# A mixture-of-experts combination and a state-space preparation inside an attention loop: each of their operations is tied to an attention unit, and their tiles move from PSUM banks to SBUF

## The chip, the cores and the metric

The kernel runs on one core of a Trainium2 chip. A core has five engines, each with its own in-order queue: PE (TensorE, matmuls), DVE (VectorE), ACT (ScalarE), POOL (GpSimd) and SP (SyncE, which here only issues DMAs). They meet at semaphores. SBUF is the working memory, PSUM holds eight banks of 128 x 512 float32 that PE writes and ACT and DVE read. The metric is the device time of one execution in microseconds, as the median of several runs.

## The reference, cut to what matters

A tensor `x` of 4 elements (the batch) by 1024 tokens by 128 features goes through four layers. Each layer is an attention-like block and a feed-forward block, each with a residual and a layer norm behind it. The change lies in the third layer and at the start of the fourth:

```
# third layer: attention (16 heads of 64), causal, relu features times cos and sin
x = layernorm(x + cosformer(x))
# third layer: mixture of experts, top 2 of 8
probs = softmax(x @ router.T); weights, indices = top_k(probs, 2)
weights = weights / (weights.sum() + 1e-6)
y = sum over the 2 chosen of weights * (silu(x @ gate_e) * (x @ up_e)) @ w2_e
x = layernorm(x + y)
# fourth layer: a selective state-space block
xn = x * rsqrt(mean(x*x) + 1e-5) * norm_w
xs = silu(conv4(xn @ in_w.T) + conv_b)           # 256 channels, 4 taps along time
delta = softplus(xs @ wd1.T @ wd2.T + wd2_b)
h[t] = exp(delta[t] * A) * h[t-1] + delta[t] * xs[t] * Bm[t]   # 16 states per channel
y[t] = sum over states of h[t] * Cm[t]
```

## The kernel before

Everything is float32. The four elements live in SBUF as `xN[b]` (tokens on partitions, 8 chunks of 128 tokens) and `xT[b]` (features on partitions). The program is written as Python generators that are advanced in turn; a scheduler with a timeline model then fixes the order of each engine's queue, moving an operation ahead of others on its engine where it holds it to be ready. Inside the attention loop PE's order alone is kept as written (`manual_schedule`).

**The attention loop** (`l2_attn`, L947) runs over 128 units: 4 elements x 4 quarters of 256 tokens x 8 pairs of heads. A unit's steps are spread over neighbouring turns `t`: `l2_project` (L1070) makes queries and keys with two PE matmuls into a bank `pqk` and two ACT activations `r_q`, `r_k` (L1078), and POOL turns the queries (`qt`, L1086); `l2_keys` transposes the keys (`kN`, L1101); `l2_scores` multiplies keys by queries into `pa_m` and DVE masks them (`a`, L1144); `l2_sums` updates the running state (matmuls into `kp_mo`, DVE `st`, L1125 and L1128); `l2_before` and `l2_within` accumulate `po` (L1153); `l2_out` divides on DVE (`dn`, `co`, L1196 to L1198). Every fourth unit `l2_project_out` transposes `co` into a bank `pt`, copies it with ACT (`coT`, L1220) and multiplies it by the output weights (`pr`, L1223). At the end of an element there is a layer norm (`norm_parts`, L162, whose Sqrt on ACT, L177, needs a table load, L177, and another, L1517, for the Tanh after it), a router and the expert dispatch.

PSUM in the loop: two rotating banks with the tag `pj` serve `pqk`, the values `pv`, the transposes `pt`, the router and everything of the early preparation below; `po` has two banks' width, `pr` one, and three shared banks hold scores, states and the experts' `ph` and `py`. PE waits for a `pj` bank until its last reader is done.

**The experts** (`l2_ffn`, L1429, the generator `moe`) start inside the attention loop as soon as an element's rows are dispatched: one expert tile of 128 rows per turn (`sg`, `mh` on DVE and ACT, L1517 to L1521, `ys`, L1537). When an element's 23 tiles are done, its **combination** `l2_combine` (L1546) follows: two halves of 4 chunks. For each half POOL issues 8 indirect DMAs that gather the two expert rows of each token (`yg`, L1556), ACT scales each of the 8 tiles of 128 x 128 by its weight (L1573, L1580), DVE adds them and the residual (L1583, L1585), and `norm_parts` makes the layer norm.

**The early preparation** (`l3_early`, L1721, and `l3_prepare`, L1745) makes the first half (512 tokens of element 0) of the fourth layer ready while the attention of element 3 still runs. It starts when element 0's combination is done, and advances by one step per unit (L1014 to L1018). Steps: squares, Sqrt and scaling (L1754 to L1761); a transpose and `xnT`; for each of two channel groups a matmul `pxe`, a four-tap convolution on DVE that reads the bank four times (L1786, L1792), three small operations for the next half's edge (`tail`), Tanh back into the bank (L1806), and `xs` (L1807); a matmul `pdb` and the store of 32 rows to DRAM; then, for each group, softplus: a matmul `pd`, Abs and a maximum, Exp, plus one, minus one back into the bank, Ln, three additions in the bank and a product on DVE (L1837 to L1840), and a copy out of the bank (L1841).

**The fourth layer** (`l3`, L1622) scans 8 halves of 512 tokens; for each of 16 states POOL multiplies (`db`, L1876), ACT takes the exponential (`da`, L1880), DVE scans (L1881), POOL multiplies again (`hc`, L1892) and PE sums in `pys`. The remaining expert tiles, the combinations of elements 1 to 3 and the last feed-forward block (`ph`, `hh`, `py`) run beside it.

The attribute `self.beat` is set in `l2_project` to the ACT instruction that makes the newest `r_k`. Before the change only the dispatch's scatters use it: they get a dependency on the beat, so that they can't be scheduled ahead of the unit at which they are written.

Of the kernel before, what the change touches and what calls it, by code (L numbers as in the profile page):

```python
# [42 lines left out]
E3, NST, DDELTA, KCONV = 256, 16, 64, 4  # L43
# [28 lines left out]
class Net:  # L72
# [874 lines left out]
    def l2_attn(self, load, dispatch, moe, first):  # L947
# [5 lines left out]
        nc, tc = self.nc, self.tc  # L953
        NQ = 2
        with ExitStack() as ctx:
# [35 lines left out]
            for t in range(-2, n + 4):  # L991
                if t == 0:
                    load()
                if 0 <= t + 1 < n:
                    u = units[t + 1]
                    if u["hp"] == 0:
                        i = (t + 1) // NP2
                        if i + 1 < len(quarters):
                            nxt = quarters[i + 1]
                            self.l2_tiles(nxt, quarters[i])  # L1000
                            side.append(self.l2_values(nxt))
                    self.l2_keys(u)
# [522 lines left out]
    def l2_expert_out(self, u, units, i, wp):  # L1525
# [12 lines left out]
        if j % 4 == n - 1:  # L1538
# [4 lines left out]
                in_=ys[:, 0:n, :],  # L1543
            )

    def l2_combine(self, st, wp):  # L1546

        nc, b = self.nc, st["b"]
        yg = {}

        def gather(h, c):
# [169 lines left out]
    def l3_early(self, pool):  # L1721


        half = lambda b, i: self.xT[b][:, i * 512 : (i + 1) * 512]
        k = [0]

        def at(name, shape):
            if name in ("xnT", "tail", "xs3"):
                return pool.tile(shape, F32, name=name)
            if name in ("dl", "ud"):  # L1730
# [8 lines left out]
            return half(0, name == "sp_w")[:, None, :]  # L1739

        u = dict(b=0, h=0, at=at, ff=self.bank("pj"))
        self.c3["first"] = u
        return u

    def l3_prepare(self, u):  # L1745
# [2 lines left out]
        at, ff, dp = u.get("at", self.l3_at), u.get("ff", self.bank("ff")), c3["dp"]  # L1748
        wdb = c3["we"][:, :, 0:ND]

        sq = at("sq3", [P, 4, D])
        ms = self.sm.tile([P, 4], F32, name="ms3")
        for k in range(4):
            nc.scalar.activation(  # L1754
                sq[:, k, :], self.xN[b][:, 4 * h + k, :], AF.Square, accum_out=ms[:, k : k + 1]
            )
        yield
        nc.scalar.activation(ms, ms, AF.Sqrt, bias=self.epsc, scale=1.0 / D)
        nc.vector.reciprocal(ms, ms)
        for k in range(4):  # L1760
            nc.scalar.activation(  # L1761
                sq[:, k, :], self.xN[b][:, 4 * h + k, :], AF.Copy, scale=ms[:, k : k + 1]
            )
        yield
        pt = ff([P, 4, P], "pt")
        for k in range(4):
            self.tr(pt[:, k, :], sq[:, k, :])
# [2 lines left out]
            xnT, pt.rearrange("p a b -> p (a b)"), AF.Copy, scale=self.col("norm_w")  # L1770
        )
        yield

        K1 = KCONV - 1
        tail = at("tail", [P, 2, K1]) if h == 0 else u["prev"]["tail"]
# [2 lines left out]
        for ec in range(2):  # L1778
            p = ff([P, 512], "pxe")
            self.mm(p, c3["wskip"][:, 1, ec * P : (ec + 1) * P], xnT)  # L1780
            xc = at("xc", [P, 512])
# [4 lines left out]
            nc.vector.tensor_scalar(xc[:, o:], p[:, o:], w[K1], bias, ALU.mult, ALU.add)  # L1786
            if h:
                nc.vector.scalar_tensor_tensor(
                    xc[:, 0:K1], p[:, 0:K1], w[K1], tail[:, ec, :], ALU.mult, ALU.add
                )  # L1790
            for d in range(1, KCONV):
                nc.vector.scalar_tensor_tensor(  # L1792
                    xc[:, d:], p[:, 0 : 512 - d], w[K1 - d], xc[:, d:], ALU.mult, ALU.add
                )
# [11 lines left out]
            nc.scalar.activation(p, xc, AF.Tanh)  # L1806
            nc.vector.scalar_tensor_tensor(xs[:, ec, :], p, 1.0, xc, ALU.add, ALU.mult)  # L1807
# [9 lines left out]
        yield  # L1817

        dl, ud = at("dl", [P, 2, 512]), at("ud", [P, 2, 512])
        for g in ((0,), (1,)) if "at" in u else ((0, 1),):  # L1820
            us, v = at("sp_u", [P, len(g), 512]), at("sp_w", [P, len(g), 512])
            p2 = []
            for k, ec in enumerate(g):
# [11 lines left out]
            for k, ec in enumerate(g):  # L1835
# [6 lines left out]
            if g[-1] == 0:  # L1842
                yield
        u.update(xnT=xnT, xs=xs, dl=dl, ud=ud, rows=rows)

    def l3_scan(self, u):
# [400 lines left out]
```

## Time and profile before

| | |
|---|---|
| median of 3 runs | 2261.67 us (2253.73 to 2262.74) |
| profiled execution | 2265.2 us; its span (first to last instruction) 2263.4 us |
| mean granted TensorE clock | 0.934 |
| PE, DVE, ACT, POOL busy | 1988.1, 1361.8, 1184.6, 1025.0 us |
| first two layers | 0 to 593 us: PE busy 505.95 us |
| attention loop of the third layer | 593 to 1303 us: PE busy 652.14 of 709.60 us |
| from there to the first `db` of the scan | 1303 to 1363.5 us: PE busy 35.82 of 60.50 us |
| scan stage | 1363.5 to 2130 us: PE 673.13, POOL 675.18 of 766.50 us |
| rest of the last feed-forward block | 2130 to 2263.4 us |

How to read the views. A row of the stretches gives, for each window of the span, its length and every engine's busy time with the number of instructions, then the granted clock of PE as a share of full speed. A row of the waits says which operation waited for which, the time in total, how often, and the longest. A row of the groups gives line, engine, operation, output and inputs, shape, count, then busy time and mean ns of one, then the idle time of the engine in front of them. A row of the timeline gives start, duration, engine, line and operation. An average over the span hides that the stages have different limits, so a change in the attention loop is read from the stretches of that loop.

Below, "element 2's twin" of a stretch means the same run of units one element earlier: the first `r_q` (L1078) of 32 units earlier starts the twin. Elements 2 and 3 do the same attention work, the same dispatch and the same expert tiles beside it; element 3's stretch has the combination and the preparation of element 0 on top.

### The profile page before, as it was taken

How to read it: one execution, taken by the hardware profiler on the slowest of the kernel's cores; microseconds unless marked ns; L12 is line 12 of the kernel's file. 1: busy time of each engine (PE TensorE's matmuls, PEld its weight loads, DVE VectorE, ACT ScalarE, POOL GpSimd, SP SyncE). 2: the span in 40 equal slices, each digit the busy share in tenths (PEclk: the TensorE clock that was granted, in tenths of full speed). 3: DMA queues.
4: the chain of work that ended last, by engine and by line, in shares of the span. 5: the costliest groups of instructions: out<-in, count | busy, mean ns of one | idle time of the engine just before them, and what ended most of it. 6: DMA issues, size and time to landing. Idle time of an engine off the chain costs nothing.

```text
span 2263.4 us, 46328 instructions
## 1 busy us (share of the span) xinstructions
PE 1988.1 (88%) x17791; PEld 1392.3 (62%) x17791; DVE 1361.8 (60%) x3705; ACT 1184.6 (52%) x2578; POOL 1025.0 (45%) x813
## 2 busy tenths in 40 slices
PE   6778889899999999999979866688898999999998
PEld 3565555544577777787768654356565656565666
DVE  7767644433455654754555555696877688686522
ACT  6532434322344444454555556476768787676443
POOL 5100411000123244234143339989788889789400
PEclk9778979889999999999999987799999999999999
DMA  3010110050000000031222066466776676676421
GB/s 107 0 38 10 31 38 1 23 172 0 2 3 2 14 27 22 25 91 41 78 79 81 17 193 193 127 193 191 205 209 172 185 186 190 181 203 170 113 61 52
DMA packets 138605, 211.04 MB, mean 93 GB/s; under 512 B 18645, under 2 KB 75982, under 8 KB 137999
## 3 DMA queue, kind: packets, MB, share of 16 engines
q1 hardware_dynamic: 126238, 173.81, 25.4%
q0 software_dynamic: 12144, 34.26, 7.3%
q8 instruction: 140, 2.29, 0.4%
q14 instruction: 83, 0.67, 0.1%
HBM read 160.22 MB, written 23.16 MB: 81 GB/s over the span
## 4 chain that ended last, share of the span: by engine, by line
PE 44%; DVE 13%; ACT 10%; issue 3%; DMA 2%; POOL 1%; SPq 0%; DVEq 0%; ACTq 0%; POOLq 0%
PE py L140 8%; PE ph L140 7%; PE po L1153 5%; DVE db L1881 5%; PE pa_m L140 5%; PE pqk L140 5%; PE kp_mo L140 3%; PE pr L1223 2%; PE pys L140 2%; PE pv L140 2%; PE pt L144 1%; ACT da L1880 1%; ACT hh L2007 1%; PE kp_mo L144 1%; ACT xN L187 1%
## 5 line engine op out<-in xcount | busy, mean ns | idle before, releaser
L1086 POOL TENSOR_TENSOR qt<-r_q,sb_c_turn 128x256 f32<-128x256 f32 (+1 forms) x256 | 164.7, 664 | 451.0 <-ACT r_q L1078 447.1
L1892 POOL TENSOR_TENSOR hc<-db,cn 128x1024 f32<-128x1024 f32 x128 | 319.0, 2529 | 67.4 <-PE pys L140 26.8
L140 PEld LDWEIGHTS py<-wh,hh 128*128 128x128 f32 x2048 | 257.0, 196 | 79.8 <-issue 47.8
L1876 POOL TENSOR_TENSOR db<-ud,bn 128x1024 f32<-128x1024 f32 x112 | 293.1, 2679 | 7.6 <-ACT dl L1841 5.1
L140 PE MATMUL ph<-xT,wh 128*128 128x512 f32 x512 | 252.9, 611 | 24.0 <-ACT hh L2007 6.7
L140 PE MATMUL py<-wh,hh 128*128 128x128 f32 x2048 | 263.8, 280 | 10.8 <-ACT hh L2007 4.2
L2007 ACT ACTIVATE hh<-ph,sb_cols 128x512 f32<-128x512 f32 x256 | 170.3, 681 | 118.3 <-PE ph L140 92.1
L1144 DVE TENSOR_TENSOR a<-pa_m,sb_c_near 128x256 f32<-128x256 f32 x256 | 96.7, 419 | 201.4 <-PE pa_m L140 201.4
L1101 ACT ACTIVATE kN<-kp_mo,sb_c_trig 128x128 f32<-128x128 f32 x448 | 130.2, 372 | 130.6 <-PE kp_mo L144 122.4
L1880 ACT ACTIVATE da<-dl,aneg 128x512 f32<-128x512 f32 x224 | 153.6, 689 | 74.4 <-DVE db L1881 73.7
L140 PE MATMUL pys<-hc,sb_c_ident 128*128 128x512 f32 x324 | 160.6, 625 | 21.3 <-POOL hc L1892 17.9
L1881 DVE TENSOR_TENSOR_SCAN db<-da,carry,db 128x512 f32<-128x512 f32 x128 | 156.9, 1265 | 21.5 <-POOL db L1876 11.2
L1881 DVE TENSOR_TENSOR_SCAN db<-da,db 128x512 f32<-128x512 f32 x128 | 149.4, 1206 | 11.5 <-ACT da L1880 6.4
L140 PEld LDWEIGHTS ph<-xT,wh 128*128 128x128 f32 x512 | 88.0, 194 | 104.3 <-issue 49.0
L2032 DVE SCALAR_TENSOR_TENSOR h_acc<-py,gt,h_acc 128x128 f32<-128x128 f32 x252 | 70.8, 343 | 123.7 <-PE py L140 123.7
L140 PE MATMUL pqk<-xT,wE 128*128 128x256 f32 x512 | 136.4, 389 | 8.2 <-ACT coT L1220 4.2
L140 PEld LDWEIGHTS pys<-hc,sb_c_ident 128*128 128x128 f32 x324 | 61.1, 201 | 83.8 <-issue 57.7
L140 PEld LDWEIGHTS pqk<-xT,wE 128*128 128x128 f32 x512 | 88.5, 193 | 21.9 <-DVE cv L1063 8.1
L1220 ACT COPY coT<-pt 128x512 f32<-128x512 f32 x64 | 37.5, 587 | 116.8 <-PE pt L144 116.8
L140 PE MATMUL po<-ht,wD 128*128 128x512 f32 x192 | 92.9, 594 | 0.0
L1153 PE MATMUL po<-cv,a 128*64 128x65 f32 x2048 | 88.3, 228 | 0.0
L1556 POOL DMA_INDIRECT yg<-yrows,di x64 | 61.3, 957 | 57.5 <-DVE ch L1388 36.7
(463 smaller groups left out, 4255.2 us busy)
## 6 DMA issues: line engine op xcount, KB each, us to landing
wx<-in_wF SPq DMA_DIRECT2D x92, 384.0 KB, 3.4
bn<-rows SPq DMA_DIRECT2D x128, 256.0 KB, 4.7
cn<-rows SPq DMA_DIRECT2D x128, 256.0 KB, 4.2
wh<-in_wH SPq DMA_DIRECT2D x64, 512.0 KB, 3.8
hc<-hc POOLq DMA_DIRECT2D x47, 512.0 KB, 7.0
xrows<-zero SPq DMA_DIRECT2D x4, 1472.0 KB, 12.0
xg<-xrows SPq DMA_DIRECT2D x20, 256.0 KB, 3.6
yrows<-ys SPq DMA_DIRECT2D x20, 256.0 KB, 3.4
```

Of the source, the lines that this page charges most:

```text
L140: return self.nc.tensor.matmul(out=out, lhsT=lhsT, rhs=rhs, start=start, stop=stop)
L1086: nc.gpsimd.tensor_mul(u["qt"][:, m, a:], u["q"][:, a:], c2["turn"][:, m, o + a : o + 2 * P])
L1101: self.nc.scalar.activation(u["kN"][:, c, m, :], pk[:, c, :], AF.Copy, scale=trig[:, k, m : m + 1])
L1144: nc.vector.tensor_mul(u["a"][:, i, :, :], pa[i], self.c2["near"][:, None, :].to_broadcast([P, 2, P]),)
L1153: self.nc.tensor.matmul(out=u["po"][self.HALF[j], i, c, :], lhsT=lhsT, rhs=rhs, start=key not in u["begun"], stop=True, skip_group_check=True,
L1556: nc.gpsimd.indirect_dma_start(out=yg[h][:, k, c, :], out_offset=None, in_=st["out"][:, :], in_offset=bass.IndirectOffsetOnAxis(ap=st["des ...
L1876: nc.gpsimd.tensor_mul(db, ud, bc[0])
L1880: nc.scalar.activation(da, dl[:, ec, :], AF.Exp, scale=aneg[:, j : j + 1])
L1881: nc.vector.tensor_tensor_scan(db[:, ec, :], da, db[:, ec, :], carry[:, ec, n : n + 1] if h else 0.0, ALU.mult, ALU.add,)
L1892: nc.gpsimd.tensor_mul(hc, db, bc[1])
L2007: nc.scalar.activation(ht, ph, AF.Relu, bias=self.col("h_b1", i=e * NK + k))
L2032: nc.vector.scalar_tensor_tensor(acc[:, c, :], py[:, c, :], gt[:, c, e : e + 1], acc[:, c, :], ALU.mult, ALU.add,)
```

## The change

- `pace(i)` is new: it gives an instruction a dependency on `self.beat`, the newest `r_k`.
- `l2_combine_first` replaces `l2_combine` for element 0. All 16 gathers (each paced) run over 8 steps; three steps after its gathers a chunk is added into `x` on DVE, with the weight as the scalar operand of two `scalar_tensor_tensor` operations (paced) in the place of ACT's scaling; statistics per chunk; then one Sqrt over all 8 chunks, one reciprocal, and the normalization of the 8 chunks, half on ACT and half on DVE, two chunks a step. `moe` is still advanced once per unit, and two steps of a combination are made at each.
- The early preparation gets more steps and every ACT and most DVE operations are paced; it is now advanced twice per unit (a second `next(begin, None)` at the end of the turn). The convolution reads an SBUF copy `e_tmp` that ACT makes of the bank. Softplus works in SBUF tiles `e_sp_u`, `e_sp_w`, `e_tmp`: the bank is read by Abs and the maximum only; Ln is taken once for both channel groups; the additions end in `dl` itself and the copy out of the bank is gone. For the later halves (`early` false) nothing changes.

```diff
@@ l2_attn
                     if next(g, self) is self:
                         side.remove(g)
+                if begin is not None:
+                    next(begin, None)
@@ new
+    def pace(self, i):
+        self.tc.add_manual_dep(i.ins, self.beat.name, SYNC, reason="spread out")
+        return i
+
+    def l2_combine_first(self, st):
...
+        def add(c):
+            for k in (1, 0):
+                self.pace(
+                    nc.vector.scalar_tensor_tensor(
+                        x[:, c, :], yg[:, k, c, :], st["wts"][k][:, c : c + 1], x[:, c, :],
+                        ALU.mult, ALU.add,
+                    )
+                )
+            v = self.sm.tile([P, 4, 6], F32, name="ln_st")
+            nc.vector.bn_stats(v[:, 0, :], x[:, c, :])
+            nc.vector.bn_aggr(mv[:, c, :], v[:, 0, :])
+
+        for c in range(NC + 3):
+            for k in range(2 if c < NC else 0):
+                self.pace(
+                    nc.gpsimd.indirect_dma_start(
...
+            if c >= 3:
+                add(c - 3)
+            yield
+        yield
+        self.pace(nc.scalar.activation(rs, mv[:, :, 1], AF.Sqrt, bias=self.epsc))
+        yield
+        yield
+        self.pace(nc.vector.reciprocal(rs, rs))
+        nc.vector.scalar_tensor_tensor(nm, mv[:, :, 0], -1.0, rs, ALU.mult, ALU.mult)
...
+        for c in range(0, NC, 2):
+            self.pace(nc.scalar.activation(x[:, c, :], ...))
+            self.pace(nc.vector.tensor_scalar(x[:, c + 1, :], ...))
+            yield
+        st["done"] = True
@@ l2_combine
+        if b == 0:
+            yield from self.l2_combine_first(st)
+            return
@@ l3_prepare
+        early = "at" in u
+        pace = self.pace if early else (lambda i: i)
...
             self.mm(p, c3["wskip"][:, 1, ec * P : (ec + 1) * P], xnT)
+            if early:
+                t = at("tmp", [P, 512])
+                nc.scalar.copy(t, p)
+                p = t
+                yield
...
-        for g in ((0,), (1,)) if "at" in u else ((0, 1),):
+        if early:
+            yield
+            us, v = at("sp_u", [P, 2, 512]), at("sp_w", [P, 2, 512])
+            t = at("tmp", [P, 2, 512])
+            for ec in range(2):
+                p = ff([P, 512], f"pd{ec}")
+                self.mm(p, c3["wd2"][:, ec * P : (ec + 1) * P], db[0 : DDELTA + 1, :])
+                nc.scalar.activation(us[:, ec, :], p, AF.Abs)
+                nc.vector.tensor_single_scalar(dl[:, ec, :], p, 0.0, ALU.max)
+                yield
+                pace(nc.scalar.activation(us[:, ec, :], us[:, ec, :], AF.Exp, scale=-1.0))
+                pace(nc.scalar.activation(v[:, ec, :], us[:, ec, :], AF.Identity, bias=self.ones[:, 0:1]))
+                yield
+            for ec in range(2):
+                pace(nc.scalar.activation(t[:, ec, :], v[:, ec, :], AF.Identity, bias=c3["neg1"]))
+            yield
+            pace(nc.scalar.activation(v, v, AF.Ln))
+            for ec in range(2):
+                yield
+                d = dl[:, ec, :]
+                pace(nc.vector.tensor_sub(t[:, ec, :], us[:, ec, :], t[:, ec, :]))
+                pace(nc.vector.tensor_add(d, d, t[:, ec, :]))
+                pace(nc.vector.tensor_add(d, v[:, ec, :], d))
+                pace(nc.vector.tensor_mul(ud[:, ec, :], xs[:, ec, :], d))
+        for g in () if early else ((0, 1),):
```

More of the change, by code (lines that the diff above doesn't have):

```diff
@@ L1544, in l2_expert_out @@
             )
+    def pace(self, i):
+        self.tc.add_manual_dep(i.ins, self.beat.name, SYNC, reason="spread out")
+        return i
+    def l2_combine_first(self, st):
+        nc, b, md = self.nc, st["b"], self.m2["md"]
+        yg = md.tile([P, 2, NC, D], F32, name="yg0")
+        mv = md.tile([P, NC, 2], F32, name="mv0")
+        rs = md.tile([P, NC], F32, name="rs0")
+        nm = md.tile([P, NC], F32, name="nm0")
+        x = self.xN[b]
+        def add(c):
[13 more added lines that the diff above has]
+                    nc.gpsimd.indirect_dma_start(
+                        out=yg[:, k, c, :],
+                        out_offset=None,
+                        in_=st["out"][:, :],
+                        in_offset=bass.IndirectOffsetOnAxis(
+                            ap=st["dest"][k][:, c : c + 1], axis=0
+                        ),
+                    )
+                )
+            if c >= 3:
[10 more added lines that the diff above has]
+        for c in range(0, NC, 2):
+            self.pace(
+                nc.scalar.activation(
+                    x[:, c, :], x[:, c, :], AF.Identity, bias=nm[:, c : c + 1], scale=rs[:, c : c + 1]
+                )
+            )
+            self.pace(
+                nc.vector.tensor_scalar(
+                    x[:, c + 1, :], x[:, c + 1, :], mv[:, c + 1, 0:1], rs[:, c + 1 : c + 2],
+                    ALU.subtract, ALU.mult,
+                )
+            )
+            yield
+        st["done"] = True
@@ L1729, in at @@
                 return pool.tile(shape, F32, name=name)
+            if name in ("sp_u", "sp_w", "tmp"):
+                return self.m2["md"].tile(shape, F32, name=f"e_{name}")
             if name in ("dl", "ud"):
@@ L1738, in at @@
                 return half(0, k[0] % 2)
-            return half(0, name == "sp_w")[:, None, :]
         u = dict(b=0, h=0, at=at, ff=self.bank("pj"))
@@ L1753, in l3_prepare @@
         for k in range(4):
-            nc.scalar.activation(
-                sq[:, k, :], self.xN[b][:, 4 * h + k, :], AF.Square, accum_out=ms[:, k : k + 1]
+            pace(
+                nc.scalar.activation(
+                    sq[:, k, :], self.xN[b][:, 4 * h + k, :], AF.Square, accum_out=ms[:, k : k + 1]
+                )
+            )
+            if early and k == 1:
+                yield
+        yield
+        pace(nc.scalar.activation(ms, ms, AF.Sqrt, bias=self.epsc, scale=1.0 / D))
+        if early:
+            yield
+        pace(nc.vector.reciprocal(ms, ms))
+        for k in range(4):
+            if early and k % 2 == 0:
+                yield
+            pace(
+                nc.scalar.activation(
+                    sq[:, k, :], self.xN[b][:, 4 * h + k, :], AF.Copy, scale=ms[:, k : k + 1]
+                )
             )
         yield
[L1758 to L1764, printed above, removed]
+        if early:
+            yield
         pt = ff([P, 4, P], "pt")
@@ L1772, in l3_prepare @@
         yield
+        if early:
+            yield
         K1 = KCONV - 1
@@ L1780, in l3_prepare @@
             self.mm(p, c3["wskip"][:, 1, ec * P : (ec + 1) * P], xnT)
+            if early:
+                t = at("tmp", [P, 512])
+                nc.scalar.copy(t, p)
+                p = t
+                yield
             xc = at("xc", [P, 512])
@@ L1785, in l3_prepare @@
             o = K1 if h else 0
-            nc.vector.tensor_scalar(xc[:, o:], p[:, o:], w[K1], bias, ALU.mult, ALU.add)
+            pace(nc.vector.tensor_scalar(xc[:, o:], p[:, o:], w[K1], bias, ALU.mult, ALU.add))
             if h:
@@ L1791, in l3_prepare @@
             for d in range(1, KCONV):
-                nc.vector.scalar_tensor_tensor(
-                    xc[:, d:], p[:, 0 : 512 - d], w[K1 - d], xc[:, d:], ALU.mult, ALU.add
+                if early and d == 2:
+                    yield
+                pace(
+                    nc.vector.scalar_tensor_tensor(
+                        xc[:, d:], p[:, 0 : 512 - d], w[K1 - d], xc[:, d:], ALU.mult, ALU.add
+                    )
                 )
@@ L1804, in l3_prepare @@
             yield
-            nc.scalar.activation(p, xc, AF.Tanh)
-            nc.vector.scalar_tensor_tensor(xs[:, ec, :], p, 1.0, xc, ALU.add, ALU.mult)
+            pace(nc.scalar.activation(p, xc, AF.Tanh))
+            if early:
+                yield
+            pace(nc.vector.scalar_tensor_tensor(xs[:, ec, :], p, 1.0, xc, ALU.add, ALU.mult))
+            yield
+        if early:
             yield
@@ L1819, in l3_prepare @@
         dl, ud = at("dl", [P, 2, 512]), at("ud", [P, 2, 512])
-        for g in ((0,), (1,)) if "at" in u else ((0, 1),):
+        if early:
+            yield
+            us, v = at("sp_u", [P, 2, 512]), at("sp_w", [P, 2, 512])
[5 more added lines that the diff above has]
+                nc.vector.tensor_single_scalar(dl[:, ec, :], p, 0.0, ALU.max)
+                yield
+                pace(nc.scalar.activation(us[:, ec, :], us[:, ec, :], AF.Exp, scale=-1.0))
+                pace(
+                    nc.scalar.activation(
+                        v[:, ec, :], us[:, ec, :], AF.Identity, bias=self.ones[:, 0:1]
+                    )
+                )
+                yield
+            for ec in range(2):
+                pace(
+                    nc.scalar.activation(t[:, ec, :], v[:, ec, :], AF.Identity, bias=c3["neg1"])
+                )
+            yield
+            pace(nc.scalar.activation(v, v, AF.Ln))
+            for ec in range(2):
+                yield
+                d = dl[:, ec, :]
[4 more added lines that the diff above has]
+        for g in () if early else ((0, 1),):
             us, v = at("sp_u", [P, len(g), 512]), at("sp_w", [P, len(g), 512])
@@ L1841, in l3_prepare @@
                 nc.scalar.copy(dl[:, ec, :], p)
-            if g[-1] == 0:
-                yield
         u.update(xnT=xnT, xs=xs, dl=dl, ud=ud, rows=rows)
```

## The prediction

> **What bounds the kernel now.** I read the page first, for the place.
>
> ```profile
> PE   6778889899999999999979866688898999999998
> ...
> PEclk9778979889999999999999987799999999999999
> ```
>
> A slice is 56.6 us. PE is the fullest engine, and in the attention loop (slices 11 to 23) it stands at nine tenths until element 0's combination starts in slice 21. The loop is bound by PE as long as DVE and ACT answer in time, so what the change can win is the time in which PE was held up. I cut element 3's part of the loop by stage, from one unit's first `r_q` to another's:
>
> ```profile
> 1135.80:1187.00 51.20, 37.20 (x522) 29.75 (x518) 28.29 (x123) 30.24 (x90) 22.47 (x28) 0.90 0.29 83
> 1187.00:1239.80 52.80, 50.06 (x864) 42.54 (x860) 29.33 (x102) 27.86 (x84) 19.48 (x26) 1.00 0.31 87
> 1239.80:1276.50 36.70, 32.96 (x659) 26.23 (x652) 22.46 (x68) 16.16 (x43) 16.83 (x21) 1.00 0.06 18
> 1276.50:1295.90 19.40, 12.28 (x168) 9.07 (x162) 7.79 (x19) 13.20 (x23) 3.81 (x5) 0.78 0.06 18
> ```
>
> and element 2's twin of each:
>
> ```profile
> 942.30:975.90 33.60, 32.17 (x530) 26.68 (x523) 23.18 (x96) 15.98 (x51) 7.21 (x12) 1.00 0.28 76
> 975.90:1028.60 52.70, 49.95 (x860) 42.43 (x856) 29.34 (x102) 27.89 (x84) 20.84 (x28) 1.00 0.32 90
> 1028.60:1061.10 32.50, 31.11 (x620) 25.01 (x616) 16.45 (x54) 12.46 (x37) 17.01 (x23) 1.00 0.06 18
> 1061.10:1069.50 8.40, 8.08 (x174) 6.80 (x174) 3.30 (x12) 3.73 (x10) 3.81 (x5) 1.00 0.14 43
> ```
>
> Columns: window, length, busy us of PE, weight loads, DVE, ACT, POOL, granted clock, DMA. Lengths differ by 17.6 us (combination), 0.1, 4.2 (convolution) and 11.0 (softplus): **32.9 us** is all that element 0's extra work costs in the loop before 1295.9, and the ceiling of the gain. PE's clock falls to 0.90 and 0.78 there and not in the twins. What held PE, in the first stretch:
>
> ```profile
> PE kp_mo L140 <- DVE st L1128: 11.3, 5, 3.7
> ACT yg L1573 <- DMA yg<-yrows,di: 7.6, 5, 2.8
> DVE yg L1583 <- ACT yg L1580: 6.2, 2, 3.3
> DVE ln_rs L178 <- ACT ln_sd L177: 6.1, 2, 4.9
> ```
>
> A chain: gathers land, ACT stands in its queue waiting for them (7.6 us, and 2.8 more at L1580), DVE waits for ACT's scaled tiles with the unit's `st` behind it, and PE waits for `st`. In the last stretch it is the `pj` banks:
>
> ```profile
> PE pqk L140 <- ACT coT L1220: 3.6, 2, 3.2
> PE pt L144 <- DVE co L1198: 3.5, 1, 3.5
> ```
>
> The additions in the bank `pd` and their Ln stand in front of `co` and `coT` (timeline: `pd` is made at 1273.8 and last read by ACT's copy at 1283.2), and two banks serve everything.
>
> **What moves and stays.** PE's order inside the loop is written by hand; the early preparation's five steps on PE shift by one unit only. In POOL's queue the 16 gathers stand where they stood, except that `qt` of one unit falls behind four of them; `qt` is wanted two turns later, so its slack hides it. The dispatch's scatters stay. In SP's queue the store of `rows` keeps its place; some later `bn` loads fall behind one expert load each, from the fifth on, and are wanted after 1393 us, while they were issued by 1376. The first `db` of the scan stands on POOL behind 8 gathers and 16 scatters of element 3's dispatch, which follow the last layer norm of the loop; so whatever the loop saves should arrive there whole, and the rest of the kernel, PE-bound at 591.45 of 650 us from 1480 to 2130, keeps it.
>
> **Cost of what is there after the change.** Durations are from these groups and their neighbours:
>
> ```profile
> L1518 DVE SCALAR_TENSOR_TENSOR sg<-sg,pa_m 128x128 f32<-128x128 f32 x50 | 13.7, 285 | 14.1 <-ACT sg L1517 13.3
> L1517 ACT ACT_TABLE_LOAD x6 | 7.7, 1283 | 0.1
> L191 DVE TENSOR_SCALAR xN<-yg,ln_mv,ln_rs 128x128 f32<-128x128 f32 x4 | 1.6, 448 | 0.0
> L1792 DVE SCALAR_TENSOR_TENSOR xT<-pxe,cw,xT 128x510 f32<-128x510 f32 x2 | 1.5, 750 | 0.1
> ```
>
> Combination: DVE 16 additions x 0.285 + 8 statistics x 0.28 + 8 aggregates x 0.163 + 0.34 + 4 normalizations x 0.448 = 10.2 us; ACT 4 normalizations x 0.485 = 1.9, and Sqrt with its two loads 0.30 + 2 x 1.283 = 2.9. Gone: 16 scalings x 0.407 = 6.5 us of ACT, and one of two Sqrt pairs; but the preparation's Sqrt, which shared a pair, now has its own.
> Preparation up to 1295.9: ACT 4 squares x 0.49 = 2.0, its Sqrt pair 2.9, 4 copies x 0.39 = 1.6, `xnT` 0.69, two new bank copies x 0.587, two Tanh x 0.60, `pdb` 0.69, Abs 2 x 0.60, Exp 2 x 0.63, plus one 2 x 0.73: 14.2 us; DVE per group 0.81 + 3 x 0.75 + 0.71 for the edge + 0.69 for `xs` = 4.46, twice, and two maxima x 0.69: 10.3, and 0.2 for a reciprocal.
> Sum 39.5 us of engine time, of which 6.1 with the two added load pairs.
>
> What a microsecond of it costs on the path is read from before. The convolution stretch cost 4.2 us for 13 us of such instructions (9.6 on DVE, 3.3 on ACT: the tanhs, `pdb`, `xnT`, Abs), 0.32. A unit with a dispatch step (931.6) against its twin (982.3): 0.6 us for 2.3, 0.26. Units that hold table loads cost more: 1225.4 against 1199.2 is 2.6 us for 4.5 (0.58), 839.9 against 801.2 is 2.3 for 2.75 (0.84). So 33.4 x 0.32 = 10.7 (bounds 0.26 and 0.58: 8.7 to 19.4) and 6.1 x 0.7 = 4.3 (3.5 to 5.1).
>
> **The added wait.** The paced additions stand on DVE, and behind a late gather would queue `dn`, `co`, `st` and then PE. In the trace the gathers are 1.25 us apart on POOL and the eighth, issued at 1147.61, is read by 1150.8; three steps are one and a half units of 6 to 8 us. Only the first three chunks are close (the second tile is read at 1143.56, its place on DVE is after the dispatch's `chd` at 1142.8). I take 1.5 us; bounds 0 and the 10.4 us that ACT waited. The wait for the beat itself costs nothing: the `r_k` named is ACT's newest, and the next `a` and `dn` follow it anyway.
>
> **Softplus at the end.** After 1295.9 come the minus ones 2 x 0.69, one Ln of double width 1.26 between two loads 2.57, and 8 DVE operations x 0.69: 10.7 us, where before 1.9 of ACT (copy, load) and 1.4 of DVE stood: 7.4 more, nearest to 0.4 because one burst of loads is in it: 3.0 (0.26 to 0.7: 1.9 to 5.2). The bank is freed by Abs and the maximum, so the 7.1 us of bank waits have no cause left; next late is `sg`, behind the Ln on ACT, priced here.
>
> **Sum.** 32.9 - 10.7 - 4.3 - 1.5 - 3.0 = 13.4 us, from +18.8 to -7.2 at the bounds. The profiled execution was 2265.2 (span 2263.4), 3.5 above the median; from the median 2261.67 this gives **2248.3**.
>
> A rule against the change: the Trainium skill, "SBUF — State Buffer", section "Who interferes with whom", says that a DVE instruction with two SBUF inputs contends with a GpSimd instruction that reads SBUF, and the later one waits; a DVE copy in a two-port mode does too. The trace agrees, with `qt` on POOL:
>
> ```profile
> 1136.41 1.42 POOL L1086 TENSOR_TENSOR qt<-r_q,sb_c_turn 128x256 f32<-128x256 f32 x2 [3.86 <-ACT r_q L1078]
> 1136.92 0.24 DVE L1316 COPY tend<-tend 128x2 f32<-128x2 f32 x1
> 1137.27 0.59 DVE L1316 COPY tend<-tend 128x4 f32<-128x4 f32 x1
> ```
>
> Some 32 operations lose their PSUM input or are new with two SBUF inputs; by the rule, with `qt` busy 1.42 of 6 us and a mean wait of half of 0.71, that is an estimate of 2.7 us more on DVE, 0.9 on the path, and the sum would be 2249.2.
>
> **The rivals.** *More*: loads and additions hide in a PE-bound loop, ratio 0.26 throughout, no gather wait: 16 to 22 us, 2240 to 2246. For it: the clock returns to 1.00. *Less*: additions wait for gathers as ACT did (10.4), or the loads' ratio holds for all work: gain 0 to 8, up to the bound 2269. For it: DVE is nearer to PE than ACT was. *The other side*: the gain is lost in the scan. The queues there are ordered anew; POOL alternates `hc` and `db` in other places, and each `hc` waits for DVE's scan.
>
> ```profile
> L1892 POOL TENSOR_TENSOR hc<-db,cn 128x1024 f32<-128x1024 f32 x128 | 319.0, 2529 | 67.4 <-PE pys L140 26.8 <-DVE db L1881 21.2 <-DVE prl L1257 3.6
> ```
>
> 67.4 over 128 is 0.53 us each. At 0.63 the gain is gone (13 us); at 0.73 the kernel takes 2274. Against it: the groups of four at the scan's start are the same, and the alternation exists before. *The change does nothing* would need the scheduler to keep the bursts; the queues of the changed program show one or two chunks per unit, so I give that nothing apart.
>
> **The numbers.** Forecast (8 to 16 us, 2246 to 2254) 0.47, more 0.17, less 0.16, other side 0.20. About 0.5%, 11.3 us, is what this kernel's runs can tell: faster means below 2250.4, which takes 0.29 of the forecast and all of "more": 0.46; slower, above 2273: 0.20; same 0.34. The range reaches from 2238 (bound 18.8, less half the runs' 9 us spread) to 2269, and leaves the other side out.
>
> **What would show it.** Right: DVE's wait on ACT in the combination gone, PE's wait for `st` near the twin's 1.2 us, clock 1.00 throughout, the stretch 1135.8 to 1187 at 38 to 42 us, the last at 10 to 13. Wrong: DVE waiting on `yg` DMAs, `sg` late by over 4 us behind the Ln, or a later scan stage with more POOL idle than before.

## The result, and the profile after

The changed kernel takes **2270.45 us** (median of 15 runs, 2265.97 to 2274.17) against 2261.68 us before (15 runs, 2253.73 to 2267.79): ratio **1.0038**, 95% interval 1.0027 to 1.0049. It is slower by 8.8 us, where I had forecast 13.4 us of gain, and lies above my range. The profiled execution took 2268.69 us, its span 2266.9.

The page of the changed kernel, its row of PE in slices of 56.7 us:

```profile
PE   6778889899999999999988856688898889898998
```

In slices 21 and 22, where element 0's combination lies, a seven and a nine have become two eights; in the scan stage slices 32, 33, 35 and 37 have fallen from nine to eight. The stretches of the loop, cut at the same units as before (columns as there: window, length, busy us of PE, weight loads, DVE, ACT, POOL, clock, DMA):

```profile
1135.40:1181.40 46.00, 35.46 (x530) 28.94 (x524) 31.09 (x126) 16.07 (x51) 22.63 (x28) 0.93 0.32 90
1181.40:1237.00 55.60, 51.06 (x875) 43.13 (x871) 31.07 (x109) 38.04 (x106) 19.45 (x26) 1.00 0.30 85
1237.00:1273.70 36.70, 31.26 (x613) 24.68 (x609) 22.15 (x66) 15.25 (x41) 18.87 (x21) 1.00 0.05 15
1273.70:1284.80 11.10, 10.48 (x194) 7.99 (x193) 4.68 (x14) 7.29 (x18) 3.80 (x5) 1.00 0.13 37
```

Over element 2's twins these cost 12.4, 2.9, 4.2 and 2.7 us: 22.2 where it was 32.9. So the loop from the combination to the last `r_q` gained 10.7 us. The whole balance, from the two traces:

| | before | after | difference |
|---|---|---|---|
| last `r_q` of the loop | 1295.9 | 1284.8 | -11.1 (0.4 of it from before the combination) |
| from there to the end of the last `po` | 9.7 | 14.9 | +5.2 |
| from there to the first `db` of the scan | 57.9 | 59.2 | +1.3 |
| halves 1 to 4 of the scan | 392.5 | 391.3 | -1.2 |
| **fifth half** (first `db` to the next half's) | 94.6 | 107.9 | **+13.3** |
| from there to the end | 412.8 | 408.8 | -4.0 |

Three things went wrong: the loop gained 5.7 us less than I summed, 5.2 us were given back at once where the sum had 3.0, and the scan lost some 8 to 13 us (8.1 from its first `db` to the end of the span, 13.3 in the fifth half alone). Together the two traces differ by 3.5 us; the other 5 of the 8.8 us come from which execution was traced, since the one of before lay 3.5 us above its median and the one of after 1.8 below.

**The five units of the combination.** The waits in the first stretch:

```profile
PE kp_mo L140 <- DVE st L1130: 8.5, 5, 3.2
DVE xN L1565 <- DMA yg<-yrows,di: 1.6, 1, 1.6
```

ACT's waits for gathers and DVE's waits for ACT are gone, as I had said; but PE's wait for `st` is 8.5 us, where I expected the twin's 1.2 (before: 11.3). The timeline of DVE, POOL and PE in one unit shows why (start, duration, engine, line, operation):

```profile
1147.15 2.59 DVE L1565 SCALAR_TENSOR_TENSOR xN<-yg,wt,xN 128x128 f32<-128x128 f32 x3
```

```profile
1148.18 1.41 POOL L1088 TENSOR_TENSOR qt<-r_q,sb_c_turn 128x256 f32<-128x256 f32 x2
```

```profile
1151.53 1.22 PE L140 MATMUL kp_mo<-wx,mh 128*128 128x128 f32 x4 [3.21 <-DVE st L1130]
1152.54 1.91 PE L140 MATMUL pv<-wE,xT 128*128 128x512 f32 x2
```

Three additions, which take 0.34 us each when nothing lengthens them, stand in front of `dn`, `co` and `st`; the third of them alone takes 2.06 us, until 1149.75, just behind the end of POOL's `qt`. PE stands 3.2 us, and then its clock is 0.50 from 1152.5 to 1157.2: the two `pv` matmuls take 1.91 us (1.02 in the twin).

**Behind the last `r_q`.** ACT's timeline:

```profile
1287.01 1.28 ACT L1941 ACT_TABLE_LOAD   x1
1288.30 1.06 ACT L1941 ACTIVATE e_sp_w<-e_sp_w 128x1024 f32<-128x1024 f32 x1
1289.38 1.28 ACT L1519 ACT_TABLE_LOAD   x1
1290.67 0.45 ACT L1519 ACTIVATE sg<-pa_m 128x128 f32<-128x128 f32 x2
```

In front of these rows stand the two minus ones (`e_tmp`, 1285.65 to 1287.0). The expert tile's `sg` (its matmuls ended at 1287.4) stands 3.3 us behind this burst, `mh` stands behind DVE's softplus operations, and PE waits 1.6 us for `mh`.

**The scan.** The group of `hc`, and the windows of the fifth half, before and after:

```profile
L2019 POOL TENSOR_TENSOR hc<-db,cn 128x1024 f32<-128x1024 f32 x128 | 315.0, 2485 | 74.8 <-PE pys L140 25.9
```

```profile
1756.00:1850.60 94.60, 88.59 (x439) 57.65 (x438) 73.66 (x144) 75.36 (x142) 81.53 (x41) 0.99 0.67 182
```

```profile
1750.20:1858.10 107.90, 92.60 (x437) 61.41 (x436) 74.39 (x144) 78.57 (x147) 81.62 (x42) 0.95 0.62 167
```

POOL does the same work (81.5 us) in 13.3 us more; the idle time in front of `hc` has grown from 67.4 to 74.8 us.

### The profile page after: what moved, and what is told of

Same layout as the page of the kernel before. It is cut to its first block, busy times and chain, and to the rows that moved or that the text cites. A ratio compares the mean times of both kernels' runs of the same rounds, so it can differ in the third digit from the quotient of the medians.

```text
span 2266.9 us, 46321 instructions
## 1 busy us (share of the span) xinstructions
PE 1983.1 (87%) x17791; PEld 1387.5 (61%) x17791; DVE 1367.5 (60%) x3715; ACT 1174.3 (52%) x2558; POOL 1026.2 (45%) x813
## 4 chain that ended last, share of the span: by engine, by line
PE 44%; DVE 14%; ACT 9%; issue 3%; DMA 2%; POOL 1%; SPq 0%; DVEq 0%; ACTq 0%; POOLq 0%
PE py L140 8%; PE ph L140 7%; PE po L1155 5%; PE pqk L140 5%; DVE db L2008 5%; PE pa_m L140 4%; PE pys L140 3%; PE kp_mo L140 3%; PE pr L1225 2%; PE pv L140 2%; PE pt L144 1%; ACT da L2007 1%; ACT hh L2134 1%; PE kp_mo L144 1%; POOL db L2003 1%
## 5 line engine op out<-in xcount | busy, mean ns | idle before, releaser
L2019 POOL TENSOR_TENSOR hc<-db,cn 128x1024 f32<-128x1024 f32 x128 | 315.0, 2485 | 74.8 <-PE pys L140 25.9
L2003 POOL TENSOR_TENSOR db<-ud,bn 128x1024 f32<-128x1024 f32 x112 | 287.6, 2610 | 8.6 <-ACT dl L1970 5.1
L140 PE MATMUL ph<-xT,wh 128*128 128x512 f32 x512 | 253.4, 611 | 30.9 <-ACT hh L2134 10.5
L2008 DVE TENSOR_TENSOR_SCAN db<-da,carry,db 128x512 f32<-128x512 f32 x128 | 157.1, 1267 | 10.5 <-ACT da L2007 10.2
L2008 DVE TENSOR_TENSOR_SCAN db<-da,db 128x512 f32<-128x512 f32 x128 | 149.3, 1206 | 10.7 <-POOL db L2003 5.6
L140 PE MATMUL pa_m<-r_q,r_k 64*64 64x128 f32 x2048 | 86.2, 283 | 1.6 <-DVE mh L1523 1.6
```

The lines of the kernel that those rows point to most:

```text
L140: return self.nc.tensor.matmul(out=out, lhsT=lhsT, rhs=rhs, start=start, stop=stop)
L2003: nc.gpsimd.tensor_mul(db, ud, bc[0])
L2008: nc.vector.tensor_tensor_scan(db[:, ec, :], da, db[:, ec, :], carry[:, ec, n : n + 1] if h else 0.0, ALU.mult, ALU.add,)
L2019: nc.gpsimd.tensor_mul(hc, db, bc[1])
```

## The experiments

From the first half of the scan on, both kernels write down the same 5160 instructions in the same sequence; only the queues that the scheduler made of them differ. So an order can be carried from one kernel to the other: each instruction is told to follow the one in front of it in a recorded order of its engine, with no wait added. "Order of before" and "order of after" mean these recorded orders from the scan on; the loop in front keeps its own. Four batches were run. In the first and the last every kernel took about 40 us more, the kernel before too (2300.1 and 2294.8 us, against 2253.9 and 2258.4 in the others), so ratios go to the kernel before of the same batch, and stretches are compared within a batch as far as there are traces; where they are not, I say so.

### Two loops by two orders

```diff
+def keep_order(tc, start):
+    by = {number from the scan's first: instruction}
+    for queue in ORDER:               # PE, ACT, DVE, POOL, SP
+        for was, now in zip(queue, queue[1:]):
+            tc.add_manual_dep(by[now], by[was].name, NoSync)
```

> The changed kernel up to the first half of the scan, but from the scan on every engine's queue is tied, instruction by instruction, to the order that the scheduler chose for the kernel before (the same 5160 instructions are written there in both kernels). Theory O (the 13 us lost between 1750 and 1858 us come from the queues' new order): the fifth half takes about 95 us as before instead of 107.9, the lead of 4.6 us at the first db grows or stays, 2254 to 2258 us, ratio about 0.997 to 0.998. Theory P (the loss is physical: transfers and expert tiles that come 5 us earlier collide): the fifth half stays at 105 to 108 us and the time at 2268 to 2272. Theory N (the order is noise on both sides): something between, 2260 to 2266.

Measured: ratio **1.0000** (0.9984 to 1.0017), fifth half 93.0 us.

> The kernel before, with the changed kernel's queue order from the scan on. Theory O: it loses in the fifth half what the changed kernel lost there, about 10 to 13 us, and takes 2271 to 2275 us (ratio 1.004 to 1.006). Theory P: the order has nothing to do with it, 2260 to 2264 us, fifth half 94 to 96 us.

Measured: ratio **1.0057** (1.0037 to 1.0077), fifth half 108.8 us.

> The changed kernel itself, its own order written down (the queues are the same), on the chip of the other runs: it completes the table of two loops by two orders. Expected from the runs so far: 1.0038 as at first, a fifth half of 107 to 109 us; and if order and loop add up, its ratio is that of before_order_of_after (1.0057) times that of after_order_of_before (1.0000), 1.0057 within their intervals of 0.002.

Measured: ratio **1.0050** (1.0032 to 1.0068), fifth half 109.4 us.

| ratio, fifth half | order of before | order of after |
|---|---|---|
| loop of before | 1, 94.6 us (first trace) | 1.0057, 108.8 us |
| loop of after | 1.0000, 93.0 us | 1.0050 and 1.0038, 109.4 and 107.9 us |

Behind either loop the order of after costs 0.4 to 0.6%, 9 to 13 us; theory P falls. And the second thing that I expected did not come: with the order held, the changed loop gains nothing that the runs of this batch can tell (1.0000, not 0.997). In this batch the five units of the combination took 53.8 us with the changed loop and 54.5 with the loop of before, where the first traces had 46.0 and 51.2. From the first `r_q` of the combination to the first `db` it takes 230.7 and 232.4 us here; in the traces of the second and third batch and the first two it takes 222.4 to 223.5 us with the changed loop and 226.2 to 228.9 with the loop of before. So the loop's gain at the first `db` is 3 to 6 us where PE is not held up as in this batch, about 0.2%, and less here.

### Which queue

```diff
 gate_behind_scans: the recorded order of after, in which
-DVE: ln_nm, th, scan, scan, scan, scan
+DVE: ln_nm, scan, scan, scan, th, scan
-ACT: th, hh, da
+ACT: da, th, hh
```

> The kernel before, with POOL's queue alone in the changed kernel's order from the scan on, every other queue as before. If the loss of the fifth half is made by POOL's order (24 of its 40 instructions there stand up to two places elsewhere: db and hc alternate singly where before they came in runs), it loses 8 to 13 us, ratio 1.004 to 1.006, the fifth half takes 104 to 109 us. If PE's and ACT's order makes it (PE waits 20 us for hh there), 0 to 3 us.

Measured: ratio 1.0093 (1.0070 to 1.0116), but the fifth half takes 92.2 us; the loss lies in the third, 123.5 us (103.8 in the profile of before).

> The complement: PE, ACT, DVE and SP in the changed kernel's order from the scan on, POOL as in the kernel before. If PE's and ACT's order makes the loss, ratio 1.004 to 1.006 and a fifth half of 104 to 109 us; if POOL's does, 0.999 to 1.001 and 93 to 96 us. If both have to stand in one order, both of these two kernels lose.

Measured: ratio 1.0124 (1.0102 to 1.0146), fifth half 110.8 us; the second half takes 94.9 (87.2 before).

Mixed orders fit each other worse than either whole one, as the last sentence of that expectation allowed. For the fifth half both runs say the same: POOL's order isn't its cause, and my theory that the alternation of `db` and `hc` makes it falls.

> The changed kernel with its own order, in which two instructions of the scan stage stand elsewhere: on DVE the gate's th of the fourth half (queued in front of the fifth half's first scans) goes behind the third of them, on ACT one da goes in front of the th, as in the order of before. If this one pair makes the loss of the fifth half (the scans stood 13 us behind a Tanh, its table load and a layer norm), the fifth half falls from 108-109 us to 94 to 99 us and the ratio to before from 1.004-1.005 to 0.998 to 1.001. If PE's py matmuls that stand in front of unready hh make it as well, 102 to 106 us and 1.002 to 1.004.

Measured: ratio 1.0041 (1.0027 to 1.0054), fifth half 106.0 us, against 107.9 and 109.4 in the two traces of the changed kernel, which are of other batches: 1.9 to 3.4 of some 15 us. The ratio is not told from the changed kernel's (1.0038 and 1.0050).

> The changed kernel with its own order up to the fifth half, and from what is written in the fifth half on all five queues in the order of before. If the loss is made by the order inside that half, it takes 93 to 97 us instead of 108 to 109 and the ratio to before is 0.994 to 0.998. If it is inherited from the order of the halves before it (th of the fourth half stays where it was), 103 to 108 us.

Measured: ratio 1.0001 (0.9986 to 1.0016), fifth half 96.6 us.

> The changed kernel with its own order; only PE's instructions around the fifth half (the expert products ph and py, the sums pys, the preparation behind them) stand as in before. If PE made the loss, py standing in front of ready work while it waits for hh (20 us of such waits against 4), 95 to 99 us. If ACT and DVE make it, 105 to 109 us. If each makes a part, 99 to 104 us.

Measured: ratio 1.0034 (1.0017 to 1.0051), fifth half 106.1 us.

> pe_order_in_fifth and gate_behind_scans together. If the two add up, the fifth half is 3 to 4 us shorter than with PE's order alone; if both are one loss seen from two queues, no shorter than the better of the two (106.0 or what PE's order gives).

Measured: ratio 1.0048 (1.0030 to 1.0067), fifth half 104.3 us, 1.8 less than with PE's order alone.

> The changed kernel with its own order; ACT and DVE alone stand as in before from the fifth half's instructions on. If ACT's place for hh among the exponentials da decides (hh late, PE waits), 96 to 101 us; if PE's order decides, 104 to 109 us.

Measured: ratio 1.0039 (1.0026 to 1.0051), fifth half 104.8 us.

So the loss is made by the order from that half on (all five queues: 96.6 us), and by no one queue that was tried: of the 12.2 us between it and the 108.8 us of the order of after (before_order_of_after, of the first batch, which ran about as long), PE's order gives back 2.7 and ACT's and DVE's 4.0. ACT's order alone, and PE's and ACT's together, were not run, so which instructions make most of the loss stays open. One part of it can be seen on DVE at the half's start, with the order of after (after_again) and of before (adds_and_ln, below):

```profile
1761.59 0.69 DVE L2055 SCALAR_TENSOR_TENSOR th<-th,psk 128x512 f32<-128x512 f32 x1 [4.79 <-ACT th L2054]
1762.20 6.79 DVE L2008 TENSOR_TENSOR_SCAN db<-da,db 128x512 f32<-128x512 f32 x6
```

```profile
1749.27 2.33 DVE L2023 TENSOR_TENSOR_SCAN db<-da,db 128x512 f32<-128x512 f32 x2
```

The first exponential `da` was done by 1748.1 in the one and by 1737.5 in the other, the half's first `db` by 1748.7 and 1740.9. With the order of before the scans follow at 1749.3, right behind a layer norm; with that of after they stand behind the layer norm, which ends at 1756.8 there, and then behind a gate `th`, which waits for the layer norm's four `xN`, two `hh`, a table load and a Tanh on ACT, until 1762.2. Counted from the start of the half's first `db`, the scans begin 16.0 us later with the order of after and 10.9 with that of before. But this is the small part: in five_queues_from_fifth the gate still stands in front (the scans begin 15.2 us after the first `db`), and the half takes 96.6 us. The larger part goes with the waits of PE and POOL, here in the fifth half of before_order_of_after and then of after_order_of_before:

```profile
PEld py L140 <- ACT hh L2007: 11.3, 7, 3.8
POOL hc L1892 <- PE pys L140: 15.0, 4, 5.6
```

```profile
PEld py L140 <- ACT hh L2134: 2.8, 5, 0.8
POOL hc L2019 <- PE pys L140: 5.6, 2, 4.1
```

PE's queue holds `py` products whose `hh` ACT has not made yet, in front of the sums `pys`; POOL waits for `pys` to free its `hc` buffers. In five_queues_from_fifth the two waits are 5.1 and 6.0 us.

### The loop, with the order held

```diff
 adds_behind_mh: in l2_combine_first
-                self.pace(nc.vector.scalar_tensor_tensor(x, yg, wts, x))
+                self.behind(nc.vector.scalar_tensor_tensor(x, yg, wts, x))  # after the newest mh, same engine
 adds_and_ln: also, in softplus
-            pace(Ln)                       # beat: the newest r_k
+            while loop is not over: yield
+            self.beat = the Sqrt of the last layer norm
+            pace(Ln); the two last DVE operations of each group
 at the loop's end, in this kernel and in tail_after_loop
-            run out begin (the preparation), then the other side tasks
+            run out the other side tasks, then begin
```

> The changed kernel with the order of before in the scan, and the sixteen additions of the first combination queued on DVE behind the newest mh of the expert tile instead of behind the newest r_k, so that they no longer stand in front of a unit's st. If they held PE there (3.2 us of waiting for st at 1148 to 1151.5 and then half a clock until 1156), the five units from 1135.4 take 39 to 42 us instead of 46.0, and the time is 4 to 7 us lower than without this edit. If the stretch is long for its DMAs or its expert tiles (loads of 2.4 MB in it), it stays at 45 to 46 us and nothing is gained.

Measured: ratio 0.9972 (0.9956 to 0.9988), against 1.0000 without the edit in the same batch. The five units took 47.8 us, not 39 to 42, and 53.8 without the edit: in both, PE stood in unit 106 (the second of the five) between matmuls with nothing to wait for that the profile shows (6.0 and 5.0 us in all; the unit took 19.3 and 17.7 us), which hides the effect. In the second batch, where it didn't, the same edit gives the window below.

> The changed kernel with the order of before in the scan, and the end of softplus (the two minus ones, Ln between its two table loads, the eight DVE operations) issued after the loop's last unit instead of in it; dl and ud are wanted only at the first db, 59 us later. If that burst is what gave back 5 us between the last r_q and the last po (14.9 us there against 9.7 before), the stretch falls to 9 to 10 us and the time lies 4 to 6 us below the changed kernel with the order of before. If the wait for sg is set by the expert tile itself, or the burst then delays the router, 0 to 2 us.

Measured: ratio 0.9990 (0.9973 to 1.0007), the stretch still 14.9 us. It tested nothing: the last `r_k` belongs to a step two turns ahead, so instructions that are written behind the loop and tied to it may start inside it, and did.

> The changed kernel with the order of before in the scan, the sixteen additions behind the newest mh as in adds_behind_mh, and Ln with the two last operations of each channel group tied to the Sqrt of the last layer norm in place of the loop's last r_k (the two minus ones and the four operations that need no Ln stay in the loop). If Ln between its loads is what made the stretch from the last r_q to the last po 14.9 us instead of 9.7, it falls to 10 to 12 us, nothing comes back later, since Sqrt, Ln and Tanh follow each other there with one load less, and the ratio to before is 0.994 to 0.996. If the norm and router behind it are delayed by as much as the loop gains, the first db comes no earlier and the ratio stays at 0.997.

Measured: ratio **0.9958** (0.9942 to 0.9973), faster than both kernels. The five units and PE's wait for `st` in them:

```profile
1133.60:1168.80 35.20, 32.43 (x530) 26.71 (x524) 28.99 (x125) 16.10 (x51) 22.51 (x28) 1.00 0.40 116
```

```profile
PE kp_mo L140 <- DVE st L1131: 1.1, 1, 1.1
```

35.2 us against 46.7 in after_again of the same batch, 1.6 over the twin; the clock stays at 1.00 and the wait for `st` is about the twin's (7.3 us in after_again). The edit does two things at once: the additions no longer stand in front of `st`, and they no longer run beside `qt`. What the sixteen take above 0.34 us each falls from 3.7 us in after_again to 0.5. So up to some 3 of the 11.5 us can be the lengthened additions themselves; no run has the one without the other. The stretch from the last `r_q` to the last `po` takes 10.7 us. ACT there:

```profile
1298.47 1.28 ACT L1959 ACT_TABLE_LOAD   x1
1299.77 1.06 ACT L1959 ACTIVATE e_sp_w<-e_sp_w 128x1024 f32<-128x1024 f32 x1
```

They follow the layer norm's Sqrt (1297.68), whose own way back to Tanh had to load a table anyway. From the last `po` to the first `db` it takes 61.1 us against 56.0 in after_again, so the 4.2 us that Ln gave came back there, as the second theory had it, but not by its norm and router: POOL's eight gathers wait until the DMA of the expert rows `yrows` has landed, at 1318.2 here and 1324.8 in after_again (32.2 and 27.2 us behind the last `po`), and from the first gather to the first `db` it takes 28.8 to 29.0 us in both. What is left at the first `db`, counted from the combination's first `r_q`, is 8.9 us of gain over after_again, less than what the additions alone gave in their five units.

> The loop of adds_and_ln with the order that the scheduler itself chooses for the scan behind it; it is a third order, unlike that of either kernel. The loop keeps its gain (35 us for the five units, 10.7 from the last r_q to the last po). If the order is a matter of luck that any change of the loop draws anew, the scan costs between 0 and 30 us more than in the order of before, and the ratio is anywhere from 0.996 to 1.010; if only the changed kernel's own timing led to the bad order, it is 0.995 to 0.997.

Measured: ratio **0.9924** (0.9904 to 0.9945), 2240.92 us against 2258.38: the best version. The scheduler's own order behind this loop has a fifth half of 92.1 us; from the last `po` to the first `db` it takes 57.9 us. It lies a little below the range of either theory. Whether the order drawn here is better than that of before isn't shown: adds_and_ln ran in another batch, the intervals overlap (0.9942 and 0.9945), and in this batch the order of before has a fifth half of 92.1 and 92.2 us behind the two loops that follow, and takes 895.4 and 890.0 us from the first `db` to the end of the span, against 894.8 here.

> The kernel before with the new combination of element 0 and the old preparation, the order of before in the scan. By the stretches of the changed kernel the combination gains 4.5 us in its five units and gives back 3 us in the eight units behind (its Sqrt and the preparation's Sqrt each load their table): ratio 0.998 to 1.000. If the combination were the larger part of the gain, as I had summed, 0.995 to 0.997.

Measured: ratio 1.0007 (0.9992 to 1.0022). The five units take 42.1 us, but the eight behind them 62.6 (52.7 before). The five units, and DVE in the one of the eight that takes longest (10.5 us):

```profile
1137.50:1179.60 42.10, 32.70 (x530) 26.74 (x526) 30.11 (x126) 16.09 (x51) 22.75 (x28) 1.00 0.34 98
```

```profile
1196.23 0.18 DVE L1826 RECIPROCAL ms<-ms 128x4 f32<-128x4 f32 x1 [2.15 <-ACT ms L1825]
```

In the five units DVE holds the additions in the same places as in the changed kernel, and PE waits 7.6 us for `st`, but the clock stays at 1.00: so of the 11.5 us that adds_and_ln saves against after_again, where the clock is 0.89, some 4.6 go with the clock and 6.9 with the wait, as an estimate from the three stretches. In the long unit the old preparation's reciprocal, which is not paced, waits on DVE for its Sqrt and the table load on ACT, in front of `co` and `st`, and PE waits 2.6 us for `st`. Before the change this Sqrt shared its loads with the combination's.

> The kernel before with the new preparation and the old combination, the order of before in the scan. By the stretches: 0 us in the convolution, 8.4 us gained at softplus before the last r_q, 5.2 us given back behind it, so 3 us in all: ratio 0.998 to 0.9995. If the 5.2 us given back belong to the expert tile and not to the Ln burst, 0.995 to 0.997.

Measured: ratio 1.0008 (0.9994 to 1.0022). Softplus takes 10.9 instead of 19.5 us before the last `r_q`, 12.0 instead of 9.7 behind it, and 63.2 us instead of 57.9 to the first `db`: of 8.6 us gained 7.6 are given back before the scan starts. Neither part alone is told from no change.

## Why the prediction was wrong, point by point

- **"whatever the loop saves should arrive there whole, and the rest of the kernel, PE-bound at 591.45 of 650 us from 1480 to 2130, keeps it"** is the step that failed, in both halves. At the first `db` 4.6 us of it were there (the loop's 11.1 less 5.2 and 1.3), and the scan's new order then took 8 to 13. I had shown no view that says how long the scan takes in another order; the loop's saving was carried over as if the queues behind it were fixed. The runs say that the order alone moves the kernel by 0.4 to 0.6%. As to the first half: POOL's gathers in front of the first `db` follow the expert rows `yrows` and not the last layer norm; after_again, adds_and_ln and adds_and_ln_own_order each show them waiting for that DMA, and the first `db` comes 25 to 29 us behind the first gather in all.
- **The other side**, at 0.20, was this mechanism, at about half the size that it names: idle time in front of `hc` grew from 0.53 to 0.58 us each over the span (74.8 over 128), 7.4 us in all. My reasons against it were true and beside the point: the first groups of four are the same, and the first half is no longer (86.3 us against 88.8); POOL's alternation isn't the cause. The loss sits in the fifth half, in how the orders of DVE, ACT and PE fit together.
- **Instructions at 0.32 of their duration.** This is the term of the sum that was mis-sized most. 10.7 us were priced by a ratio from the convolution. The five units cost 12.4 us over the twin where the sum had 4.4 to 8.4 (38 to 42 us). The additions are queued in front of the unit's own `st`, and there they cost more than their duration: 8.5 us of PE's wait and then half a clock. adds_and_ln shows it: with the same instructions behind `mh`, and no longer beside `qt`, the five units cost 1.6 us. So the kind of an instruction does not give its ratio. The ratio itself was read wrongly too: the convolution's twin makes the values of the next quarter (eight matmuls `pv` of 0.59 to 0.70 us and four additions `cv` of 0.69), and element 3, the last, has none to make. The convolution's instructions therefore cost more than the 4.2 us read there, by up to some 5 us of PE as an estimate, and the ceiling of 32.9 us is too low by as much.
- **The added wait**, 1.5 us for gathers: measured 1.6 (DVE on `yg`). Right.
- **The added load pairs**, 4.3 us for two: the eight units behind the combination, which hold both, cost 2.9 over their twin where it was 0.1. Nearly right. (The engine times as listed add to 39.7 us and the two pairs to 5.7, not 39.5 and 6.1; the forecast moves by 0.1 us.)
- **The convolution**: 4.2 us over the twin before and after. The sum named no gain there, and none came.
- **Softplus**: the stretch to the last `r_q` takes 11.1 us (said: 10 to 13), and PE's wait for `coT` fell from 3.6 to 0.6 us. Right. The tail was sized 3.0 us with a bound of 5.2; it measured 5.2: DVE's softplus operations stand in front of `mh` as well as the Ln in front of `sg`, and with Ln and the last of these operations behind the loop (adds_and_ln) it is 1.0.
- **The rule on the shared port.** I had put it aside as an estimate of 2.7 us on DVE. Summed over the DVE instructions from 1135 us to the loop's end, what each takes over the shortest of its line and shape in this stretch (0.1 us and more) is 5.6 us after and 0.8 before; all but 0.2 us of it after the change is beside `qt`. "SBUF — State Buffer", section "Who interferes with whom", in the Trainium skill, says that of two instructions which need the shared port the later one waits out the other: here 0.34 us became 0.44 to 0.81 beside `qt`. That the one addition at 1147.69 took 2.06, through two memsets and both halves of `qt`, is more than one such wait, and no run here shows why.

## What to carry to other kernels

Work that is spread thin still costs by its place: give a side task's instruction a place behind the last link of the main chain in its queue (here behind `mh`), and away from what lengthens it, not a pace alone; 11.5 us hung on that. Where a scheduler fixes the queues, compare two versions with the order of everything behind the edit held, before a difference below 1% is put down to the edit; and look through the orders that come out, since the order that the scheduler drew cost some 0.5% behind one loop and nothing that the runs can tell behind another. Tying an instruction to a beat does not keep it out of a loop whose beat runs turns ahead.

## What the hardware showed beside

Behind PE's wait of 3.2 us the window of 4.7 us that follows has half the clock:

```profile
1152.50:1157.20 4.70, 4.70 (x18) 3.67 (x17) 1.18 (x3) 0.41 (x2) 1.69 (x2) 0.50 0.44 126
```

As an estimate, the work done in it would have taken some 2.4 us less at full speed, so that wait cost about 5.5 us. "TensorE: Matmul & The Clock Gate", section "What's actually happening", in the Trainium skill, says that PE's clock is halved after an idle window of about 3.4 us and restored after a busy one. The halving is here, but the wait in front of it, 3.2 us, is shorter than that, and in the same unit of after_again PE waits only 1.85 us at once; two stretches of 3.41 us there, one behind the other:

```profile
1144.48:1147.89 3.41, 1.56 (x13) 1.37 (x13) 3.06 (x12) 0.55 (x2) 2.79 (x4) 1.00 0.13 38
1147.89:1151.30 3.41, 3.41 (x12) 2.38 (x12) 1.18 (x3) 0.27 (x1) 1.88 (x2) 0.50 0.55 169
```

PE was busy for 1.56 of the 3.41 us, and the clock was halved all the same. In combination_alone a wait of 2.2 us in the same unit left the clock at 1.00. So the length of one wait does not decide it here; what does was not tested.

In the first and last batch PE stood up to 10.5 us at single places with nothing that the profile shows (10.5 us in front of a `pxe` in tail_after_loop, 9.6 in front of a `pav` of the first two layers in adds_behind_mh), in every kernel's trace; the traces of the other two batches, and those of the two kernels before and after, show no such wait of PE. What makes it stays open, and so does what in the scheduler's model led it to the order of after: I only showed that the order, not the loop, carries the loss.
